# Pairwise products of embedded fields: stores from two queues, and another list of output slots

## The chip, the cores and the metric

The kernel runs on one core of a Trainium2 chip. The metric is the device time of one execution in microseconds (us), lower is better. The kernel before takes 1287.08 us, the median of 3 runs (1286.76 to 1287.32).

## What is computed

There are 4096 samples with 32 fields of 64 numbers each, in float32, and one 64x64 matrix W.

```
vid = jnp.einsum('bfd,de->bfe', x, W)
idx_i, idx_j = jnp.triu_indices(32, k=1)
return x[:, idx_i, :] * vid[:, idx_j, :]
```

Each sample thus gives 496 products, one for each pair of fields i < j: the field i times the transformed field j. The input is 33.6 MB, the output 520 MB, so nearly all that moves is output.

## The kernel before

**Layout.** The host stores the 64 numbers of a field down the partitions, two halves of the batch above each other, so that the 128 partitions hold 2 x 64 numbers and 128 samples lie along the free axis. A *unit* is one such block of 128 x 128 float32 values (65,536 B, 512 B in each partition). The batch makes 16 tiles. A tile's input is 32 units (one for each field), its output 496 units. All 16 tiles have 7936 output units, and the program writes them in one long row in DRAM.

**Memory.** One SBUF tile `mem` of 445 units (`UNITS`, line 17) holds both inputs and outputs; all places in it are written down by hand. `XPLACE` (line 26) gives the first unit of each tile's input. `SLOTS` (lines 29 to 40) cuts the row of 7936 outputs into slots: (units, first unit in `mem`, and, where there are more numbers, seams: points in the slot at which a VectorE operation must not run on). A slot's seam lets its first part be written while a store from the place of its second part is still under way. The places overlap: a slot goes where earlier slots and inputs no longer needed have been.

**Work of a tile** (loop over `t`). TensorE multiplies the tile by W (line 172, eight matmuls of 4 fields) into `vid`, which fills the whole PSUM. VectorE then computes the 496 products in the order of `by_block` and `products`, one instruction for a block of pairs, cut at slots and seams (line 196), straight into the slot. When the last unit of a slot has been computed, the slot is stored with one DMA (line 199): 128 rows, one from each partition, of up to 127 x 512 B.

**Loads.** The first tile comes in two DMAs (lines 136 and 140). Five more tiles follow at once (line 153, `load`): tiles 1 to 3 in one DMA, and 5 and 4 in two pieces of 38 and 26 units (`CUTS`, line 25). Tiles 6 to 10 are loaded when tile 4 has been computed, in pieces of 127, 7 and 26 units, and tiles 11 to 15 when tile 9 has been computed, in pieces of 127, 7 and 26 units. These two are called the later loads below; each is 160 units.

**Order.** All DMAs are issued by the sync engine (SP) in program order, each after what it needs: a store after the products in its slot, a load after the stores and products that used its place. SP's and VectorE's order is that of the program (`manual_schedule`, line 121). Waits between instructions follow from the regions of `mem` that each writes and reads: a product that overwrites a unit waits until the store that reads it has landed. One more wait is written out: `behind` (line 159) makes the first store after a group of load pieces wait until the second last piece has landed (lines 200 to 202). So the store comes into the queue while the last piece still runs.

The lines that the change touches are the list `SLOTS`, line 121, and the store with its wait, lines 198 to 207.

Of the kernel before, what the change touches and what calls it, by code (L numbers as in the profile page):

```python
# [26 lines left out]


SLOTS = [
    (96, 221), (120, 80), (116, 200, 21), (100, 64, 16), (92, 164, 36), (92, 256), (127, 96, 68),  # L30
    (124, 223, 33), (125, 64), (120, 191), (64, 311), (112, 79), (124, 224), (108, 64),
    (120, 176, 48), (112, 301), (120, 64), (112, 205), (120, 320), (112, 93), (127, 205), (121, 64),
    (96, 189), (120, 48), (116, 168, 21), (100, 32), (104, 132, 36), (48, 236), (124, 16),
    (127, 157, 79), (109, 0, 16), (120, 109, 48), (88, 229), (127, 16, 93), (127, 160, 69),
    (114, 0, 16), (120, 114), (112, 237), (127, 0), (121, 128), (120, 261), (127, 1), (127, 128),
    (122, 259), (120, 176), (116, 297), (92, 160, 16), (88, 252, 45), (72, 341), (120, 160, 92),
    (120, 293, 48), (32, 413), (120, 173), (126, 319), (122, 144), (127, 287, 32), (119, 128, 16),
    (126, 247), (127, 96), (109, 223), (112, 333), (127, 158), (127, 285), (127, 64, 94),
    (127, 192, 93), (124, 320), (120, 48), (127, 190), (124, 317), (125, 158),
]  # L40


# [10 lines left out]
def by_block():  # L53


    def within(lo):
        yield "step", lo, 2, 1, 0
        for k in range(2):
            yield "step", lo, 4, 2, k
        for i in (lo, lo + 8):  # L60
            yield "row", i + 4, i, 4, 4
        yield "row", lo + 8, lo, 8, 8

    yield from within(0)
    yield "row", 16, 0, 16, 16
    yield from within(16)


def products(blocks, at=0):

    for kind, a, b, c, d in blocks:
        if kind == "row":
            rows, n, i0, di, j0, dj = c, d, b, 0, a, 1
        else:
            rows, n, i0, di, j0, dj = 16 // b, c, a, b, a + c + d, b
        r = k = 0
        while r < rows:
            room = BREAKS[bisect_right(BREAKS, at)] - at
            if k or room < n:
                m, w = 1, min(n - k, room)  # L80
            else:
                m, w = min(rows - r, room // n), n
            yield at, m, w, i0 + r * di + k, di, j0 + r * dj, dj
            at += m * w
            if k + w == n:
                r, k = r + m, 0
            else:
                k += w
# [10 lines left out]
@with_exitstack  # L99
def pairwise_bilinear_kernel(  # L100
    ctx: ExitStack,
    tc: tile.TileContext,
    x0: bass.AP,
    x: bass.AP,
    out: bass.AP,
):

    nc = tc.nc
    NT = sum(len(tiles) for group in GROUPS for tiles in group)
    F = x0.shape[1] - 1 - PAD0
    D = P // 2
    NP = F * (F - 1) // 2

    BANK = 512 // C


    ctx.enter_context(tc.manual_schedule(engines={mybir.EngineType.SP, mybir.EngineType.DVE}))

    const = ctx.enter_context(tc.tile_pool(name="const", bufs=1))
    psum = ctx.enter_context(
        tc.tile_pool(name="ps", bufs=1, space=bass.MemoryType.PSUM)
    )
    vid = psum.tile([P, F, C], F32)

    mem = const.tile([P, UNITS, C], F32)


    w2 = const.tile([P, P], F32)


    place = XPLACE[0]
    nc.sync.dma_start(
        out=mem.rearrange("p u c -> p (u c)")[:, place * C - D : (place + F // 2) * C],
        in_=x0.rearrange("p u c -> p (u c)")[:, C - D : (1 + F // 2) * C],
    )
    nc.sync.dma_start(out=mem[:, place + F // 2 : place + F, :], in_=x0[:, 1 + F // 2 : 1 + F, :])  # L140
    nc.vector.memset(w2, 0.0)  # L141
    for half in (slice(0, D), slice(D, P)):
        nc.vector.tensor_copy(w2[half, half], mem[half, place - 1, C - D :])  # L143
    loaded = 1

    def load(tiles, cuts=()):
        nonlocal loaded
        n = len(tiles) * F
        place = XPLACE[tiles[0]]
        at = (loaded - 1) * F  # L150
        loaded += len(tiles)
        return [
            nc.sync.dma_start(out=mem[:, place + lo : place + hi, :], in_=x[:, at + lo : at + hi, :])  # L153
            for lo, hi in cuts or [(0, n)]
        ]

    ready = mybir.DependencyInfo(mybir.DependencyClass.Sync, mybir.DependencyReason.DATA)

    def behind(later, earlier):
        tc.add_manual_dep(later.ins, earlier.ins.name, ready, reason="issued when that has landed")  # L160

    pieces = []
    groups, cuts = iter(GROUPS), iter(CUTS)
    for tiles, parts in zip(next(groups)[1:], next(cuts)):
        pieces = load(tiles, parts)

    for t in range(NT):
        xt = mem[:, XPLACE[t] : XPLACE[t] + F, :]


        for b in range(0, F, BANK):
            nc.tensor.matmul(  # L172
                vid[:, b : b + BANK, :],
                lhsT=w2,
                rhs=xt[:, b : b + BANK, :],
                start=True,
                stop=True,
            )

        for at, m, w, i, di, j, dj in products(by_block(), t * NP):  # L180
            slot = bisect_right(STARTS, at) - 1
            n = m * w
            begin, end = STARTS[slot], STARTS[slot + 1]
            ot = mem[:, SLOTS[slot][1] : SLOTS[slot][1] + SLOTS[slot][0], :]
            o = ot[:, at - begin : at - begin + n, :]
            if m == 1:
                left = xt[:, i : i + w, :]
                right = vid[:, j : j + 1, :].to_broadcast([P, w, C])
            else:
                o = o.rearrange("p (m w) c -> p m w c", m=m)  # L190
                right = vid[:, j : j + (m - 1) * dj + 1 : dj, :].unsqueeze(2).to_broadcast([P, m, w, C])
                if di == 0:
                    left = xt[:, i : i + w, :].unsqueeze(1).to_broadcast([P, m, w, C])
                else:
                    left = xt.rearrange("p (m d) c -> p m d c", d=di)[:, i // di : i // di + m, i % di : i % di + w, :]
            nc.vector.tensor_tensor(o, left, right, ALU.mult)  # L196
            at += n
            if at == end:
                store = nc.sync.dma_start(out=out[:, begin:end, :], in_=ot)  # L199
                if pieces:  # L200
                    behind(store, pieces[-2])
                    pieces.clear()


        if t + 2 == loaded < NT:
            (tiles,) = next(groups)
            pieces = load(tiles, next(cuts))


_INS = ["r_x", "L0_rec_W"]  # L210
# [42 lines left out]
```

## Time and profile before

| | |
|---|---|
| median of 3 runs | 1287.08 us |
| the profiled execution | 1287.24 us |
| its span in the trace | 1285.5 us |
| VectorE busy | 1084.0 us |
| of it, 345 products | 1083.4 us |
| VectorE waiting for stores to land | 164.2 us, 33 times |
| TensorE busy | 231.1 us |
| SP waiting for VectorE before a store | 1104.4 us, 67 times |
| stores, loads | 70, 11, all issued by SP |
| a store from issue to landing | 19.6 / 24.6 / 38.1 us (least, median, most) |

The page of the profile gives the busy time of each engine and its share of the span; then the span in 40 slices, with a digit for the busy tenths (9 is 90% or more), the DMA engines' share and their rate; then each DMA queue with its packets, its MB and the time of its packets as a share of the 16 DMA engines' span. "SPq" is SP's issuing of DMAs. A row of an instruction group gives line, engine, operation, output and inputs with their shape, the number of instructions, then the busy time in us and the mean of one in ns, then the engine's idle time before them and what ended it. A row of a table by stretches gives the stretch, its length, the busy time and the number of instructions of each engine, TensorE's granted clock, the share of time in which the DMA engines were busy, and their rate in GB/s. A row of the timeline gives start, duration, engine, line and operation, and in brackets the idle time before it with what ended that.

### The profile page before, as it was taken

What the parts mean: (1) busy time and instruction counts of PE and PEld (TensorE: products, weight loads), DVE (VectorE), ACT (ScalarE), POOL (GpSimd) and SP (SyncE); (2) the same over time, 40 slices, a digit from 0 to 9 for tenths busy, and PEclk for the clock granted to TensorE, in tenths of its full rate; (3) what the DMA queues carried; (4) which work ended last, traced back from release to release, by engine and by line L of the source; (5) the groups of instructions that cost most, each with busy time, mean ns of one, the idle gap of its engine ahead of it and who ended that gap; (6) DMA issues with size and microseconds to landing.
All of it is one profiled execution on the core that took longest, in us unless ns stands there. A gap on an engine that the chain in (4) does not pass through costs nothing.

```text
span 1285.5 us, 1143 instructions
## 1 busy us (share of the span) xinstructions
PE 231.1 (18%) x256; PEld 67.7 (5%) x256; DVE 1084.0 (84%) x348; POOL 0.2 (0%) x4
## 2 busy tenths in 40 slices
PE   5031121303120212040311211103122130312000
PEld 1000000100000000010000000000000010000000
DVE  6889998899967389899799992849998889999952
POOL 0000000000000000000000000000000000000000
PEclk8555565556555556555565555556555555555555
DMA  9999999999999999999999999999999999999998
GB/s 400 438 429 438 436 428 438 431 435 436 432 430 439 416 433 425 445 430 433 439 427 441 435 429 436 419 432 429 440 432 440 429 430 441 429 441 430 434 436 370
DMA packets 11670, 553.75 MB, mean 431 GB/s; under 512 B 1296, under 2 KB 1296, under 8 KB 1552
## 3 DMA queue, kind: packets, MB, share of 16 engines
q1 hardware_dynamic: 11664, 553.69, 99.8%
q8 instruction: 2, 0.03, 0.0%
q14 instruction: 4, 0.03, 0.0%
HBM read 33.59 MB, written 520.09 MB: 431 GB/s over the span
## 4 chain that ended last, share of the span: by engine, by line
DVE 47%; DMA 44%; issue 6%; PE 0%; DVEq 0%; SPq 0%
DVE mem L196 47%; DMA out_dram<-mem 41%; DMA mem<-in_r_x_dram 3%; PE vid L172 0%; DVEq L241 0%; DVEq L196 0%; DVE w L143 0%; SPq L153 0%; DVEq L143 0%; SPq L199 0%
## 5 line engine op out<-in xcount | busy, mean ns | idle before, releaser
L196 DVE TENSOR_TENSOR mem<-mem,vid 128x1024 f32<-128x1024 f32 (+17 forms) x345 | 1083.4, 3212 | 170.5 <-DMA out_dram<-mem 164.2
L172 PE MATMUL vid<-mem,w 128*128 128x512 f32 x256 | 231.1, 1039 | 951.3 <-DVE mem L196 843.8
L172 PEld LDWEIGHTS vid<-mem,w 128*128 128x128 f32 x256 | 67.7, 306 | 1113.5 <-DVE mem L196 1011.9
L143 DVE COPY w<-mem 64x64 f32<-64x64 f32 x2 | 0.4, 190 | 5.0 <-DMA mem<-in_r_x_dram 4.9
L141 DVE MEMSET w<- 128x128 f32 x1 | 0.2, 165 | 0.8 <-PEq L221 0.8
L221 POOL MEMSET const-bfloat16-1.0<- 128x1 bf16 x1 | 0.1, 101 | 0.0
L221 POOL MEMSET const-uint8-127<- 128x1 uint8 x1 | 0.1, 101 | 0.0
L221 POOL MEMSET const-float32-0.0<- 128x1 f32 x1 | 0.1, 98 | 0.2 <-issue 0.2
L221 POOL MEMSET const-float32-1.0<- 128x1 f32 x1 | 0.1, 98 | 0.0
## 6 DMA issues: line engine op xcount, KB each, us to landing
out_dram<-mem SPq DMA_DIRECT2D x15, 8128.0 KB, 27.4
out_dram<-mem SPq DMA_DIRECT2D x14, 7680.0 KB, 24.9
out_dram<-mem SPq DMA_DIRECT2D x6, 7168.0 KB, 26.2
out_dram<-mem SPq DMA_DIRECT2D x5, 7936.0 KB, 28.2
out_dram<-mem SPq DMA_DIRECT2D x3, 7424.0 KB, 22.6
out_dram<-mem SPq DMA_DIRECT2D x3, 5888.0 KB, 20.9
mem<-in_r_x_dram SPq DMA_DIRECT2D x2, 8128.0 KB, 37.6
out_dram<-mem SPq DMA_DIRECT2D x2, 8064.0 KB, 24.3
```

Source lines behind the costliest of these rows:

```text
L141: nc.vector.memset(w2, 0.0)
L143: nc.vector.tensor_copy(w2[half, half], mem[half, place - 1, C - D :])
L172: nc.tensor.matmul(vid[:, b : b + BANK, :], lhsT=w2, rhs=xt[:, b : b + BANK, :], start=True, stop=True,)
L196: nc.vector.tensor_tensor(o, left, right, ALU.mult)
L221: nc = _bacc.Bacc("TRN2", target_bir_lowering=False, num_devices=1, dynamic_dma_scratch_size=512)
```

## The change

Three things change. The list of slots has 77 entries for 70, with other sizes and places. ScalarE's order is that of the program too. And the stores are issued in turn by SP and by ScalarE (`nc.scalar`), each of which has a DMA queue of its own; the turn starts with SP, and again with SP after each of the two later loads. Where load pieces came before, the first store still waits for the second last piece, and the second store now waits for the last piece. The loads stay on SP. No other engine has work on ScalarE's queue, and ScalarE computes nothing in either kernel.

```diff
 SLOTS = [
-    (96, 221), (120, 80), (116, 200, 21), (100, 64, 16), (92, 164, 36), (92, 256), (127, 96, 68),
-    (124, 223, 33), (125, 64), (120, 191), (64, 311), (112, 79), (124, 224), (108, 64),
...
-    (127, 192, 93), (124, 320), (120, 48), (127, 190), (124, 317), (125, 158),
+    (88, 229), (88, 64), (88, 152, 77), (76, 241), (88, 64), (96, 152), (100, 248), (108, 64, 88),
+    (108, 172, 76), (68, 281), (108, 64), (108, 172), (100, 281), (124, 64, 108), (124, 188),
+    (68, 313), (124, 64), (120, 188), (104, 308), (124, 64), (124, 188), (127, 317), (125, 64),
+    (96, 189), (84, 32), (80, 116, 73), (88, 197), (84, 32), (80, 117), (88, 197), (100, 0),
+    (88, 100), (96, 188), (96, 0), (104, 100, 88), (104, 208), (96, 0), (112, 96), (104, 208),
+    (120, 0), (112, 120), (112, 237), (126, 0), (122, 128), (127, 254), (121, 0), (120, 134),
+    (112, 269), (120, 197), (96, 317), (56, 160, 37), (56, 216), (64, 277, 40), (72, 341),
+    (80, 160), (88, 240), (96, 349), (80, 160), (104, 245), (96, 349), (104, 128), (112, 232),
+    (96, 344), (104, 128), (104, 232), (108, 336), (127, 96), (125, 223), (96, 348), (120, 64),
+    (127, 190), (127, 318), (122, 64), (120, 198), (127, 318), (124, 40), (125, 164),
 ]

-    ctx.enter_context(tc.manual_schedule(engines={mybir.EngineType.SP, mybir.EngineType.DVE}))
+    ctx.enter_context(tc.manual_schedule(engines={mybir.EngineType.SP, mybir.EngineType.DVE, mybir.EngineType.Activation}))

+    turn = 0
     for t in range(NT):
...
             if at == end:
-                store = nc.sync.dma_start(out=out[:, begin:end, :], in_=ot)
+                queue = nc.sync if turn % 2 == 0 else nc.scalar
+                store = queue.dma_start(out=out[:, begin:end, :], in_=ot)
+                turn += 1
                 if pieces:
-                    behind(store, pieces[-2])
-                    pieces.clear()
+                    behind(store, pieces[-2] if turn == 1 else pieces[-1])
+                    if turn == 2:
+                        pieces.clear()

         if t + 2 == loaded < NT:
             (tiles,) = next(groups)
             pieces = load(tiles, next(cuts))
+            turn = 0
```

Slots are counted from 0 in the order of the list. The first later load comes between the stores of slots 22 and 23 in the new list, the second between those of slots 47 and 48.

## The prediction

> **What bounds the kernel now.** I read the page's engine shares first, then its DMA rows, then the time in stretches.
>
> ```profile
> span 1285.5 us, 1143 instructions
> PE 231.1 (18%) x256; PEld 67.7 (5%) x256; DVE 1084.0 (84%) x348; POOL 0.2 (0%) x4
> DMA  9999999999999999999999999999999999999998
> q1 hardware_dynamic: 11664, 553.69, 99.8%
> HBM read 33.59 MB, written 520.09 MB: 431 GB/s over the span
> ```
>
> VectorE is busy for 84%, the 16 DMA engines for 99.8%, and all the bytes go through one queue, q1. The chain of waits gives DVE 47% and DMA 44%, but that only says through whom the last wait passes. What counts is that the engines never run dry. The stretches show where the rate is lost:
>
> ```profile
> core 0: us, PE busy (x) PEld busy (x) DVE busy (x) POOL busy (x), PEclk, DMA share, GB/s
> 100.00:350.00 250.00, 46.91 (x52) 13.88 (x52) 233.41 (x58) 0.00 (x0) 0.54 1.00 434
> 350.00:440.00 90.00, 14.76 (x16) 4.53 (x16) 54.90 (x21) 0.00 (x0) 0.52 1.00 428
> 500.00:780.00 280.00, 56.45 (x60) 16.02 (x60) 259.28 (x83) 0.00 (x0) 0.54 1.00 434
> 780.00:860.00 80.00, 6.34 (x8) 2.45 (x8) 41.37 (x12) 0.00 (x0) 0.52 1.00 428
> 860.00:1240.00 380.00, 68.33 (x72) 18.91 (x72) 352.17 (x118) 0.00 (x0) 0.53 1.00 434
> 1240.00:1285.50 45.50, 0.00 (x0) 0.00 (x0) 13.08 (x3) 0.00 (x0) 0.50 0.89 387
> ```
>
> The last two columns are DMA share and rate: 434 GB/s in the body, 428 around the two later loads, less only in the first microseconds and at the end. There is almost no hole to fill. A change of queues can win only if two queues raise the 434, and can lose wherever it opens a hole.
>
> **Two exchange rates.** A unit is one 128x128 float32 block, 65,536 B. The DMA engines need 65,536 B / 434 GB/s = 0.151 us for it; VectorE 1083.4 us / 7936 = 0.137 us (0.90 of that). A slot is filled, then stored; the next slot in its place may be written when the store has landed.
>
> **The queues.** 70 issues on SP become 40 on SP and 37 on ScalarE (the turn starts anew after each later load: 12 and 11, 13 and 12, 15 and 14). One takes 0.332 us (median of the store issues), 23 us in all, and SP waited 1104 us for VectorE beside them. ScalarE runs nothing else. So the issue time is hidden before and after: 0 us. The page "DMA: Bandwidth & Descriptors" of the Trainium skill, Rules for kernel authors, says that spreading DMAs over issuing engines does not help bandwidth and saves only issue time; by it alone the sum would be 0, and this trace, with one data queue, can't test it.
>
> **How two queues share the engines** is not in this trace. Two ends: the engines serve stores in the order of issue (the order as before), or they take turns, so that two stores in flight get half the rate each. Nothing in the program orders the two queues against each other, while each is in order by itself; I take turns. The same page, Queues, rings and completion order, states a round robin between queues at packet boundaries; no run shows that yet.
>
> **The list.** I worked out, for each VectorE operation, which store must have landed. Before, 47 of 70 slots hold operations that wait for the store two places back (3435 of 7936 units); after, 19 of 77 (591 units). With slots of n units and a wait for the third store back, turns leave the second store back half done and the last one whole when VectorE may go on: 1.5n units. Filling takes 0.9n. So 0.6n, about 60 units or 9 us, are left when the next store is issued. The body stays covered: 0 us. (On the old list turns would leave 0.5n against 0.9n: that would stall.) Seven more stores mean 7 x 144 packets, 63 per engine. (11,664 packets are 81 DMAs of 144: nine on each engine, eight with rows and one that marks the end.) Price: the engines' packet time is 0.998 x 1285.5 = 1282.9 us; at 437 GB/s, the best full 100 us in the trace (1100 to 1200), the 553.75 MB take 1267.2 us; the rest, 15.7 us over 729 packets, is at most 0.022 us each, so 0 to 1.4 us. I take the middle, **+0.7 us**.
>
> **The start.** Slot 0 has 88 units for 96. The first store still waits for the second last load piece (28.7 us; before it was issued at 28.78 us), and loads are in the queue until 34 us. The second store waits for the last piece, but its 88 units are done only near 40 us. Stores 2 to 8 each find an earlier one in flight by the same sums, with 1 to 4 us to spare. 0 us.
>
> **After the two later loads** the cover is thin. Before, this place looks so:
>
> ```profile
> 790.81 2.95 SPq L153 DMA_DIRECT2D mem<-in_r_x_dram  x3
> 809.19 26.54 DVE L196 TENSOR_TENSOR mem<-mem,vid 128x8192 f32<-128x8192 f32 x5 [10.50 <-DMA out_dram<-mem]
> 829.50 57.28 SPq L199 DMA_DIRECT2D out_dram<-mem  x5
> 853.05 16.48 DVE L196 TENSOR_TENSOR mem<-mem,vid 128x1536 f32<-128x1536 f32 x4 [17.32 <-DMA out_dram<-mem]
> ```
>
> SP sends the first store behind the second last piece (829.50), the next follows at 833.50, and VectorE waits until the first has landed (853.0). The second, 116 units, then covers 17.5 us, and VectorE needs 76 units, 10.4 us. In one queue nothing is lost. After the change SP issues no other store meanwhile; on ScalarE the second store waits for the last piece and then runs **beside** the first. What is queued behind these waits: on SP slot 50's store, on ScalarE slot 51's, neither computed yet. Both first stores end almost together:
>
> - Second load: slot 48 (120 units, SP) and slot 49 (96, ScalarE). Slot 50 is filled but for its last 19 units, which overlap slot 48's place: operations of 11 and 8 units, 1.61 + 1.21 us by the rows 128x1408 and 128x1024. Restart: 0.1 us from landing to VectorE (1247.04 to 1247.13 in the chain) + 2.8 + 1.0 us from issue to the first packet (first load issued at 0.73, first packets at 1.73) = 3.9 us. Cover, if the first store has one turn less to go: one of the second store's eight parts per engine, 96 x 0.151 / 8 = 1.8 us; at worst none. Loss 2.1 to 3.9 us.
> - First load: slots 23 (96) and 24 (84); slot 25 lacks its last 7 units, 1.08 us by the row 128x896. Restart 0.1 + 1.1 + 1.0 = 2.2 us, cover 0 to 1.6 us. Loss 0.6 to 2.2 us.
>
> In order of issue both losses are 0. I take turns with one part of cover: **+2.1 and +0.6 us**. Behind slot 50 the slots grow 56, 56, 64, 72, 80: each is filled in 0.137 us a unit plus about 1 us, against the one before it at 0.151, so the margins are near zero; each may add some tenths, which I leave to the range.
>
> **The end.** The last slot waits for the store three back with two others in flight, before for the one two back with a wait of 13.7 us at 1247.13. The last store was issued at 1260.24 with 24.4 us to land, 19 of them its own 125 units; so the engines had work either way. 0 us. VectorE has 308 products for 345; it is not the bound: 0 us.
>
> **Sum.** The profiled execution took 1287.24 us (span 1285.5 and 1.7 around it): 1287.24 + 0.7 + 2.1 + 0.6 = 1290.6. The median of the runs is 0.16 lower: **1290.5 us**.
>
> **Rivals** (0.2%, 2.6 us, is about what a measurement of this kernel can tell from no change):
>
> 1. Turns with thin cover: 1290.5 us, 1288.5 to 1294.5 by the ends above. For it: the overlaps in the list. Chance 0.44 (0.31 slower, 0.13 same).
> 2. The two queues don't share as I think: served by issue order, or ScalarE's issues end up in the same queue, so that the change doesn't do what it says. No stall, only the packets: 1287.6 us. For it: one queue has kept the engines 99.8% busy in order. Against it: landing in order is forced only within one queue. Chance 0.24 (0.01, 0.20, 0.03 for faster, same, slower).
> 3. Two queues raise the rate, because an engine has the other queue's packet ready while one ends. Place: the body, 860 to 1240 us and its like, price: 437 for 434 GB/s, 1275.9 - 1267.2 = 8.7 us over the 553.75 MB; it decides from 435.2 GB/s on, where it makes up the 3.4 us above. 1287.1 + 3.4 - 8.7 = 1281.8 us. For it: packets cost something beside their bytes, if at most 0.022 us each. Against it: a share of 1.00 leaves no visible gap. Chance 0.20 (0.17 faster, 0.03 same).
> 4. Two streams cost rate, as loads beside stores do in the table (428 for 434, 1.4%): up to 18 us, 1305 us. Against it: those 428 hold the small load pieces too. Chance 0.12, all slower.
>
> Faster 0.18, same 0.36, slower 0.46. The range: 1282 (rival 3 at nearly its full price) to 1297 (all ends of case 1 together and some tenths from the ramp); most of rival 4 and the far end of rival 3 stay out, some 0.15. The likeliest case's own range is 1288.5 to 1294.5.
>
> **What would show it.** Two data queues in the DMA rows with about half the stores each; stores landing some 30 us after issue where now it is 24.6, with VectorE waiting about as much as now; 434 GB/s in the body; two short holes in the DMA row some 25 to 35 us after the later loads, and VectorE waiting there for the first store, then for nothing. Issue-to-landing times as now would speak for rival 2, over 435 or under 432 GB/s in the body for rivals 3 and 4. I am wrong if holes appear in the body, where I count 9 us of cover, or if the rate moves at all.

## The result and the profile after

The kernel takes 1293.05 us (median of 5 runs, 1292.11 to 1293.41) against 1287.08 us before: 1.0047 times the time, 95% interval 1.0036 to 1.0059. It is slower, by 6.0 us. The profiled execution took 1293.35 us with a span of 1291.6 us, 6.1 us above that of before. The page of the kernel after, its span, engine shares and DMA queues:

```profile
span 1291.6 us, 1122 instructions
PE 227.3 (18%) x256; PEld 67.2 (5%) x256; DVE 1081.2 (84%) x311; POOL 0.2 (0%) x4
DMA  9999999999999999999999999989999999999998
q1 hardware_dynamic: 7344, 306.48, 55.3%
q10 hardware_dynamic: 5328, 247.20, 44.3%
```

There are two data queues now: q1 with 40 stores and 11 loads, q10 with 37 stores (51 and 37 times 144 packets). Together they keep the DMA engines busy for 99.6%, where the one queue had 99.8%. One slice of the DMA row, the 27th, shows an 8. VectorE has no more work than before and waits about as long for stores (166.2 us for 164.2). So the place of the loss is not in a sum over the whole; the same stretches as before show it:

```profile
350.00:440.00 90.00, 13.98 (x16) 4.56 (x16) 47.47 (x18) 0.00 (x0) 0.52 1.00 429
500.00:780.00 280.00, 52.55 (x56) 14.58 (x56) 258.93 (x61) 0.00 (x0) 0.54 1.00 434
780.00:860.00 80.00, 10.23 (x12) 3.70 (x12) 36.09 (x10) 0.00 (x0) 0.54 1.00 426
860.00:1240.00 380.00, 66.58 (x72) 18.84 (x72) 351.38 (x93) 0.00 (x0) 0.54 0.99 429
```

From 500 to 780 us two queues reach the 434 GB/s of one. From 860 to 1240 us it is 429 for 434. Narrower stretches, two of them beginning 9 and 14 us after the last piece of a later load has landed, first of the kernel after, then of the kernel before:

```profile
430.00:475.00 45.00, 0.00 (x0) 0.00 (x0) 29.94 (x9) 0.00 (x0) 0.50 0.98 416
465.00:780.00 315.00, 62.34 (x68) 17.55 (x68) 293.93 (x78) 0.00 (x0) 0.55 1.00 435
850.00:905.00 55.00, 9.00 (x10) 2.50 (x10) 37.93 (x18) 0.00 (x0) 0.53 0.93 396
905.00:1240.00 335.00, 57.58 (x64) 16.34 (x62) 313.45 (x76) 0.00 (x0) 0.54 1.01 435
```

```profile
430.00:475.00 45.00, 1.92 (x4) 0.53 (x2) 24.52 (x9) 0.00 (x0) 0.54 1.00 434
850.00:905.00 55.00, 14.67 (x15) 4.13 (x16) 50.93 (x23) 0.00 (x0) 0.56 1.00 433
```

The last column is the rate. Outside these two stretches it is 435 GB/s (434 and 435 before). Inside them (434 - 416) / 434 x 45 = 1.9 us and (433 - 396) / 433 x 55 = 4.7 us of transfer are missing: 6.6 us, which is the whole difference (6.1 us) within the resolution of the rates: they count a packet whole in the stretch in which it starts. With the bytes of each packet spread over the time that it took, 1.8 and 4.1 us are missing. The timeline around the larger of the two:

```profile
831.39 76.15 SPq L201 DMA_DIRECT2D out_dram<-mem  x4
836.24 83.25 ACTq L201 DMA_DIRECT2D out_dram<-mem  x4
867.07 64.91 DVE L197 TENSOR_TENSOR mem<-mem,vid 128x1408 f32<-128x1408 f32 x23 [29.37 <-DMA out_dram<-mem]
```

and the chain of waits there:

```profile
831.39 35.58 DMA out_dram<-mem
...
867.07 0.13 DVE mem L197
```

Slot 48's store (120 units) is issued at 831.39 on SP, slot 49's (96 units) at 836.24 on ScalarE. The first lands after 35.6 us, at 866.98. Alone its 120 units would need 18.1 us; both stores together, 216 units, need 32.6 us. So they have been carried side by side: on each of the 16 engines their rows follow each other in turn, one from q1, one from q10. Only now may VectorE write slot 50's last 19 units (two operations, 2.8 us), and slot 50 is issued at 869.85. The DMA rows for 866 to 874 us, forty slices of 0.2 us, show what the engines have meanwhile (their second line gives GB/s):

```profile
DMA  9505000000000000000000099000990000900009
GB/s 737 246 0 246 0 0 0 0 0 0 0 0 0 0 0 0 0 0 0 0 0 0 0 1864 430 0 0 0 1004 1290 0 0 0 0 2294 0 0 0 0 1577
```

A packet is written down where it starts, so a zero is not yet an idle engine. From 866.8 to 870.6 us no row starts; but the last rows of slot 49, which started before, run 1.8 us each (49,152 B at a sixteenth of 434 GB/s). Behind them comes, on each engine, a packet of 4 B that marks the end of the store. These marks are all that starts from 867.0 to 868.5 us:

```profile
q10 hardware_dynamic: 16, 0.00, 0.6%
```

They start between 867.1 and 868.4 us, on the mean at 867.7, and slot 49's store lands 32.5 us after its issue, at 868.7. The next rows come at 870.7, 0.8 us after the issue of slot 50. So an engine has nothing to carry for 3.0 us on the mean. That is the hole.

### The profile page after: what moved, and what is told of

It is laid out like the page before. It is cut to its first block, busy times and chain, and to the rows that moved or that the text cites. A ratio compares the mean times of both kernels' runs of the same rounds, so it can differ in the third digit from the quotient of the medians.

```text
span 1291.6 us, 1122 instructions
## 1 busy us (share of the span) xinstructions
PE 227.3 (18%) x256; PEld 67.2 (5%) x256; DVE 1081.2 (84%) x311; POOL 0.2 (0%) x4
## 4 chain that ended last, share of the span: by engine, by line
DMA 46%; DVE 42%; issue 9%; DVEq 0%; SPq 0%
DVE mem L197 42%; DMA out_dram<-mem 39%; DMA mem<-in_r_x_dram 7%; DVEq L246 0%; SPq L153 0%; DVEq L197 0%; SPq L140 0%; SPq L136 0%; SPq L201 0%
## 5 line engine op out<-in xcount | busy, mean ns | idle before, releaser
L197 DVE TENSOR_TENSOR mem<-mem,vid 128x1024 f32<-128x1024 f32 (+13 forms) x308 | 1080.6, 3582 | 171.9 <-DMA out_dram<-mem 166.2
L173 PE MATMUL vid<-mem,w 128*128 128x512 f32 x256 | 227.3, 1023 | 963.3 <-DVE mem L197 868.1
## 6 DMA issues: line engine op xcount, KB each, us to landing
out_dram<-mem ACTq DMA_DIRECT2D x5, 6144.0 KB, 29.9
```

The costliest lines, as they stand in the source:

```text
L173: nc.tensor.matmul(vid[:, b : b + BANK, :], lhsT=w2, rhs=xt[:, b : b + BANK, :], start=True, stop=True,)
```

## The experiments

Theory: two queues neither raise nor cut the rate, and the loss is the restart behind each later load, where VectorE needs the first of two stores that run side by side and end almost together. Rival A: two queues cost something on every store. Rival B: the list, with more and smaller slots, costs it.

**The new list, one queue.**

```diff
-                queue = nc.sync if turn % 2 == 0 else nc.scalar
+                queue = nc.sync
```

> The list of 77 slots with all stores issued by SP; the waits behind the load pieces as after the change. Theory (the loss is two restarts, behind the later loads, where the two first stores run side by side and end almost together): in one queue the first store lands alone and the second covers the restart, so 1287.1 + 0.6 for 63 more packets per engine = 1287.7 us (1287.0 to 1288.4), and 434 GB/s both at 430 to 475 us and at 850 to 905 us. Rival A (two queues cost something on every store): the same 1287.7 us. Rival B (more and smaller stores, or the new places, cost it): 1292 to 1293 us.

Measured: 1287.28 us, 1.0004 times before (0.9996 to 1.0013). Its stretches behind the two later loads:

```profile
430.00:475.00 45.00, 3.83 (x4) 1.00 (x4) 36.83 (x14) 0.00 (x0) 0.53 1.00 431
850.00:905.00 55.00, 14.20 (x14) 3.84 (x15) 51.65 (x22) 0.00 (x0) 0.50 1.00 433
```

The rates are 431 and 433 GB/s where 434 were expected, 0.4 us in all. The list by itself costs nothing that can be measured: rival B falls. Either the holes or the queues themselves remain.

**The first two stores behind a later load in one queue.** The turn is the only edit; 75 of the 77 stores run as in the change or with the two queues exchanged.

```diff
-                queue = nc.sync if turn % 2 == 0 else nc.scalar
+                queue = nc.scalar if (turn >= 2 if t >= 5 else turn >= 1) and turn % 2 == (0 if t >= 5 else 1) else nc.sync
```

> The change, but the first two stores behind each later load both go to SP's queue, the third to ScalarE's, and so on in turn. Theory: the first lands before the second begins, so the holes at 445 and 870 us go: 1293.05 less 1.9 and 4.7 us = 1286.5 to 1288.5 us. Rival A (two queues cost something everywhere) and rival B (the list): 1292 to 1293 us, since 75 of 77 stores are as they were.

Measured: 1287.24 us, 1.0006 times before (0.9997 to 1.0015). The timeline behind the second later load, and the two stretches:

```profile
830.49 55.60 SPq L201 DMA_DIRECT2D out_dram<-mem  x4
852.63 15.81 DVE L197 TENSOR_TENSOR mem<-mem,vid 128x1408 f32<-128x1408 f32 x6 [11.36 <-DMA out_dram<-mem]
855.41 41.74 ACTq L201 DMA_DIRECT2D out_dram<-mem  x3
```

```profile
430.00:475.00 45.00, 0.00 (x0) 0.00 (x0) 32.07 (x11) 0.00 (x0) 0.50 1.00 431
850.00:905.00 55.00, 12.01 (x12) 3.00 (x12) 47.20 (x21) 0.00 (x0) 0.56 0.99 428
```

Slot 48 lands 22.0 us after its issue where it took 35.6, VectorE goes on at 852.63, and slot 50 is issued at 855.41, while slot 49 is still under way. Where two stores stand in the queues thus carries 5.8 of the 6.0 us (5.3 by the two ratios to the kernel before). Rival A falls too: two queues still serve all the rest.

**Also at the start.**

```diff
-                queue = nc.sync if turn % 2 == 0 else nc.scalar
+                queue = nc.scalar if turn >= 2 and turn % 2 == 0 else nc.sync
```

> As the kernel with the first two stores behind each later load in SP's queue, and so too at the start (slots 0 and 1 on SP, slot 2 on ScalarE). Theory: slot 0 lands at about 47 us and not at 55.7, slot 2 is issued some 5 us earlier, and what the engines lose near 58 us goes: 0.3 to 0.8 us less than that kernel. Rivals: no difference.

Measured: 1288.10 us, 1.0009 times before (0.9999 to 1.0018). What was to happen at the start did: slot 0 lands at 47.35 us, slot 2 is issued at 49.09 for 57.34, and from 56 to 61 us the rate is 433 GB/s where the kernel that it started from has 351. But the expected gain of 0.3 to 0.8 us is not seen in the time, and the two kernels' intervals overlap, so no difference can be told.

**A longer restart.** Slots 50 and 51 change places in the list.

```diff
-    ... (56, 160, 37), (56, 216), ...
+    ... (56, 216), (56, 160, 37), ...
```

> The change with slots 50 and 51 exchanged in the list: slot 50 now lies wholly in slot 48's place, so 56 units and not 19 are left to do when slot 48 has landed. Theory (the hole at 870 us is the restart of VectorE and of the queue): a restart of 7.7 us of products in place of 2.8, so the hole grows by 4.9 us: 1293.05 + 4.9 = 1298 us (1296.5 to 1299.5). Rival (the hole comes from the queues, by the wait behind the last load piece or the empty queue, whatever VectorE does): 1293 us.

Measured: 1298.65 us, 1.0096 times before (1.0079 to 1.0113). Its stretch:

```profile
850.00:905.00 55.00, 6.22 (x6) 1.51 (x6) 37.30 (x17) 0.00 (x0) 0.50 0.85 359
```

359 GB/s for 396: 37 / 434 x 55 = 4.7 us more are missing, and the time is 5.6 us longer (6.3 by the two ratios to the kernel before). The hole follows what VectorE has to do after the landing.

**The old list, two queues.**

```diff
-    (88, 229), (88, 64), (88, 152, 77), ...
+    (96, 221), (120, 80), (116, 200, 21), ...
```

> The list of 70 slots with the stores in turn from two queues. Theory (stores in flight take turns, so a product that waits for the store two places back finds about half a slot left to cover nine tenths of a slot of work): 39 of the 70 slots hold 40 or more units that wait so; a hole of up to 0.4 x 113 units x 0.151 = 6.8 us each, half of that on the mean, 39 x 3.4 = 130 us: about 1420 us (1330 to 1500), with the rate low in the body. Rival A (a fixed cost for each store or a lower rate with two queues): 1291 to 1294 us. Rival of issue order (the queues are served in order of issue): 1287 us.

Measured: 1310.97 us (one run). Two queues with the old list do cost time, but a fifth of what I had expected. A stretch of its body, and below it, from the view of the stores, the least, median and longest time to landing (19.6, 24.6 and 38.1 us before):

```profile
465.00:780.00 315.00, 61.10 (x68) 17.59 (x68) 288.91 (x101) 0.00 (x0) 0.55 1.00 427
```

```
DMA to landing us min/median/max: 15.3/25.2/41.1
```

The rate is 427 GB/s in this stretch of the body, and 428 from 905 to 1240 us, so the loss is not only behind the loads. But the share is 1.00: in these parts of the body the engines are hardly idle, where the theory had holes; some rows take longer. At 547.7 us, for instance, where one store ends and the next begins in the other queue, the first rows, of 65,024 B, take 3.2 us on each engine, and 2.4 are enough at a sixteenth of 434 GB/s. Nor do the stores run side by side for as long as I had thought. A store is issued 7.5 us (median) before the one before it lands, much as in the one queue of before (7.2; the change has 12.5). Its 113 units need 17.1 us, so less than half of it can be done by then. My sum took the second store back as half done at every slot. That step was wrong. That the stall corrects itself, since a late VectorE issues the next store late too, is my reading of these times and not tested.

**The price of a queue and of a packet.** Three kernels store the same bytes and compute nothing; of the first, only the added loop is shown.

```diff
+    total = NT * NP
+    for turn, begin in enumerate(range(0, total, 127)):
+        m = min(127, total - begin)
+        queue = nc.sync
+        queue.dma_start(out=out[:, begin : begin + m, :], in_=mem[:, 317 : 317 + m, :])
```

> Stores alone, to measure the price of a queue and of a packet: the five first loads as they are, then 63 stores of 127 units (the last of 62) from one place, all on SP; the products and the two later loads are left out, so the output is not the products. 7936 units at 0.151 us behind 33 us of loads: 1231 us (1225 to 1240). It is the measure for the next two.

> The same stores alone (products and later loads left out), in turn from SP's and ScalarE's queue. Theory (two queues neither raise nor cut the rate, the change loses only in its holes): the time of the kernel with one queue within 0.1%. Rival A (two queues cost 0.4% by themselves): 5 us more. Rival 3 of the prediction (two queues raise the rate): up to 9 us less.

> The same stores alone (products and later loads left out), from one queue in 126 stores of 63 units: 63 stores more, 567 packets more per engine. By the prediction's price of 0.011 us each: 6 us more than with 127 units (0 to 12 by its bounds, 0 to 0.022 us).

Measured: 1235.46 us with one queue, 1236.18 us with two (in each 4 runs within 0.6 us), 1241.25 us with 126 small stores. Two queues cost 0.7 us or 0.06% over 63 stores; they don't gain. A packet costs (1241.25 - 1235.46) / 567 = 0.0102 us beside its bytes, with the end marks counted as packets. From 100 to 1100 us:

```profile
100.00:1100.00 1000.00, 0.00 (x0) 1.00 1.00 434
```

reads the same for one and for two queues.

**Loads beside stores.** Could a second queue be of use in another way? The kernel with stores alone got two loads on ScalarE's queue, and the kernel before its two later loads.

```diff
+        last = nc.scalar.dma_start(out=mem[:, 96:223, :], in_=x[:, rows : rows + 127, :])
```

> The stores alone from SP (products left out), and beside them two loads of 127 units from ScalarE's queue, right behind the first loads. Theory (the two queues share one rate, whatever the direction): 1235.5 + 254 x 0.151 = 1273.8 us (1272.5 to 1276). Rival (a load and a store run beside each other at more than 434 GB/s in all): down to 1236 us.

Measured: 1274.65 us. The 254 units cost 39.2 us, 0.154 us each, where a unit of a store needs 0.151: the rate is shared whatever the direction.

```diff
-            pieces = load(tiles, next(cuts))
+            load(tiles, next(cuts), nc.scalar)
```

> The kernel before with its list of 70 and all stores on SP; only the two later loads go to ScalarE's queue, and no store waits for their pieces. Theory (the queues share one rate, and holes alone cost time): if stores and loads cover each other at both places, 1286.5 to 1287.5 us, no difference from before; a hole there if a store half as fast frees its place too late: 1288 to 1292 us. Rival (loads and stores together run faster than 434 GB/s): 1260 to 1284 us.

Measured: 1292.06 us, 1.0041 times before (1.0028 to 1.0054). The timeline at the second later load, and its stretch, first of this kernel, then of the kernel before:

```profile
792.84 2.95 ACTq L153 DMA_DIRECT2D mem<-in_r_x_dram  x3
828.14 26.54 DVE L196 TENSOR_TENSOR mem<-mem,vid 128x8192 f32<-128x8192 f32 x5 [27.52 <-DMA out_dram<-mem]
836.86 53.47 SPq L199 DMA_DIRECT2D out_dram<-mem  x5
```

```profile
800.00:880.00 80.00, 8.07 (x10) 2.56 (x10) 49.55 (x15) 0.00 (x0) 0.54 0.94 405
800.00:880.00 80.00, 10.26 (x12) 3.45 (x12) 52.47 (x16) 0.00 (x0) 0.53 1.00 426
```

The load takes turns with the store of slot 43 of the old list, which was under way; that store lands only at 828.1 (809.1 in the kernel before), where VectorE has waited 27.5 us for the place, and the next store is issued at 836.86. From 800 to 880 us the rate is 405 GB/s for 426, so 80 x 21 / 434 = 3.9 of the 5.3 us are missing here. It is the same fault in another place: a transfer that VectorE waits for was made to share. None of these kernels beats the kernel before; the two best equal it.

## Why the prediction was right, and what was off

The forecast was 1290.5 us, slower by a stall behind each later load; measured are 1293.05 us. That is inside the range, but the loss is 6.0 us where 3.4 were forecast. By its steps:

- **The body stays covered, 0 us.** Right: 435 GB/s between and behind the two places (434 and 435 before), with 40 and 37 stores on the two queues. The median of 29.9 us from issue to landing, where some 30 us were forecast as a sign of turns, came true for another reason: the new list in one queue has 30.5 us.
- **The queues take turns.** Right: slot 48 needed 35.6 us beside slot 49 and 22.0 us before it in one queue. Rival 2 falls with that and with the second data queue, q10. The page "DMA: Bandwidth & Descriptors" of the Trainium skill, Queues, rings and completion order, has the engines go round between the queues; these landing times agree.
- **No gain in rate.** Right: rivals 3 and 4 fall with the stores alone, 1236.18 us for 1235.46. The same page's rule that spreading DMAs over engines brings no bandwidth holds here.
- **63 packets more per engine, 0.7 us.** Right: 63 x 0.0102 = 0.64 us by the small stores. In the change this is below what the rates can show.
- **The restarts, 2.1 and 0.6 us.** The mechanism was right (the longer restart and the two stores in one queue show it), the size too small: 4.7 and 1.9 us are missing by the rates, 4.1 and 1.8 us with the packets' bytes spread. The restart was sized rightly: 0.1 + 2.8 us from landing to issue, and 0.8 us instead of 1.0 from there to the first row, 3.7 us for 3.9. Two terms were off. One is the **cover**: I took one part of the second store, 1.8 us, as still to go when the first has landed. With a hole of 3.0 us it was 3.7 - 3.0 = 0.7 us. A store has landed when its last engine is done: slot 48's end marks came by 864.3 us on 14 engines and at 866.3 and 866.6 us on the other two, so most engines were well into slot 49's last row by then. At the first load the same working gives a restart of 2.0 us and a hole of 0.9 us, so 1.1 us of cover for 1.6. The other term is the **ramp**, which I had left to the range with some tenths. At 887.7 us slot 52's store begins on the 16 engines, one row of 32,768 B on each, just where slot 51's rows end:

```profile
887.70:888.00 0.30, 0.30 (x1) 0.26 (x2) 0.30 (x1) 0.00 (x0) 0.50 6.92 1748
```

The share counts the whole time of the rows that start here: 6.92 x 0.30 = 2.1 us for each, where 1.2 us are enough at a sixteenth of 434 GB/s. So 0.9 us are lost with no engine idle. Slot 26's first rows lose 0.8 us in the same way at 459.2 us (2.5 us for 1.7 on 14 engines). Holes of 3.0 and 0.9 us and slow first rows of 0.9 and 0.8 us make 5.6 us.
- **The start and the end, 0 us.** Neither is quite 0. At 58.5 us first rows of slot 2 are slow too (ten of them take 2.5 us for 1.7, 0.5 us over the 16 engines); from 56 to 61 us the rate is 351 GB/s after the change and 433 in the kernel with slots 0 and 1 in one queue. The end gained: from 1240 us on, (434 - 387) / 434 x 45.5 = 4.9 us are missing before, and with 399 GB/s over 51.6 us 4.2 us after. The two nearly cancel.
- **The aside on the old list** named the right sign but rested on a second store back that is half done at every slot; the run showed a store issued only 7.5 us (median) before the one before it landed, and 24 us lost, not the some 130 that I then worked out from it.

Two things stay open. Why the first rows of a store are slow when it is issued 1.1 to 1.5 us before the rows of the other queue end (slots 2, 26 and 52) was not measured by itself; slot 50's, which found no other store under way, took 1.07 us for 28,672 B, the full rate. And that the 6.0 us are these terms (5.6 + 0.5 + 0.6 for the packets - 0.7 at the end) is a sum with a resolution of some tenths of a microsecond.

## What to carry to other kernels

When the DMA engines are busy for 99.8%, another queue has nothing to fill, and only takes the order from the transfers: a store that frees a place for the next work should not share the engines with one that frees nothing yet. Ask at each place where production restarts (behind loads, at the start) what is still in the queue when the awaited store lands, and count the restart in full: landing to engine, the work, issue to first packet. A store lands when its last engine is done, so take the cover from where the other engines then stand. If a second queue is wanted, keep the first two transfers of a restart in one queue.

## What the runs showed of the hardware

Two transfers in different queues of one core share one rate, 434 GB/s, whether both store (1236.18 for 1235.46 us) or one loads (0.154 us for a unit, 0.151 for one of a store). On each engine the rows of two stores in different queues go in turn (slots 48 and 49). A packet of 32 to 65 KB costs 0.010 us beside its bytes. A store that is issued just before the other queue runs out lost 0.5 to 0.9 us with its first rows (at 887.7 us 2.1 us for 32,768 B). With the old list two queues lost 24 us, in part by rows that took longer (3.2 us for 65,024 B at 547.7 us).
